# Causal mask in a decoder's self-attention: from a triangle matmul on TensorE to a select on GpSimd, with values held two steps and q and k pieces given out one by one

## The chip, the core and the metric

The kernel runs on one core of a Trainium2 chip. The core has five engines with queues of their own: TensorE (PE, whose weight loads are shown apart as PEld), VectorE (DVE), ScalarE (ACT), GpSimd (POOL) and SyncE (SP), which here issues DMAs. The metric is the time of one execution on the device in microseconds; several executions give a median.

## The reference

A decoder of four layers works on x of shape 8 x 256 x 128 (batch, tokens, features), in float32. Each layer adds self-attention (or another mixer), cross attention to a context, and a feed-forward part with experts. The change concerns attention. Layers 0 and 1 have causal self-attention with 16 heads of 8 features; the core of it:

```python
    scores = jnp.einsum('bhqd,bhkd->bhqk', Q, K) * scale
    causal = jnp.tril(jnp.ones((S, S), dtype=bool))
    scores = jnp.where(causal, scores, NEG_INF)
    weights = jax.nn.softmax(scores, axis=-1)
    attn = jnp.einsum('bhqk,bhkd->bhqd', weights, V)
```

Q and K are turned by rotary tables first. Cross attention of layers 0, 1 and 3 has the same heads; layer 0 masks keys and multiplies the weights by a side input after the softmax (`attn = attn * group_prob[:, None, :, :]`), layer 1 masks keys, layer 3 has neither. Layer 2 has another kind of attention, and the self-attention place of layer 3 is a state-space scan; neither runs the changed functions.

## The kernel before

The work of attention is cut into 40 jobs, a job being one layer and one batch element: eight each of causal layer 0 (`L0a`), cross layer 0 (`L0x`), causal layer 1 (`L1a`), cross layer 1 (`L1x`), cross layer 3 (`L3x`). Layers 0 and 1 go in halves of four batch elements: L0a 0-3, L0x 0-3, L0a 4-7, L0x 4-7, and so for layer 1.

Each job goes through these generators in `main_line`:

- `fronts` and `front` (L666 to L752), for two jobs at once: normalise x, make the rows of q and k (`rows_of`), split each into three bfloat16 pieces whose sum is the float32 value (`pieces`, L641, four GpSimd operations: copy, subtract, copy, subtract), and lay the pieces out by DMA on SP's queue (`spread`, L655) into the tiles `qs` and `ks`. The score matmuls then run on bfloat16 operands of up to 128 rows.
- `pass1` (L800): the score matmuls a first time, mask included, for the row maxima, which DVE reduces from PSUM (L824). GpSimd splits the negated maxima into pieces (`mp`, L831 to L834); PE transposes them (L847), ACT copies them, and SP's queue lays them into further rows of `qs` (`all_maxima`). With these rows the matmuls of the second pass yield score minus maximum.
- `pass2` (L857): keys are now on the partitions. There are eight steps per job: four groups of four heads (`s`), two blocks of 128 keys (`kt`). A step makes banks of 512 scores (L893), takes their exponential on ACT (L901, tile `prob`) and, for `L0x`, multiplies them by the transposed side input into `probw`, in turn on DVE and GpSimd (L906). The value matmuls of a step (`values`, L867) are issued one step later: the step is kept in `held`. In causal jobs the second key block needs the second 128 queries only; in both blocks the first 128 query columns of a bank are the diagonal block. There a matmul of the identity with `tri_k` (L896), a triangle of 0 and -1e30, adds the mask to the scores in PSUM, as `tri_q` does in `pass1` (L818).
- `terms` (L761): loads the masks of cross layers (and the side input), turns a mask into a matmul operand on GpSimd (`mq`, L774 or L776), and transposes it on PE (L758).
- `backs`: normalises and projects out.

The order of work is written out by Python generators, not by the chip. `drive` (L392) emits one unit of `pass1` or of `pass2` at a time; `pass1` leads by about 1.15 job (`LEAD`), and a clock counts the units. The other generators, among them fronts, terms, backs and the experts of other layers (`aside`), advance when their own time has come: `yield us(t)` sets a pause of t microseconds on that clock (`TICK` 0.85 us per unit), a bare `yield` sets 1.8 us. Emission fixes the order in each engine's queue, so a pause moves instructions past others, and takes no time on the chip by itself.

Tiles come from rotating buffers: `sb(shape, tag, bufs)`. `prob` has 6 and `probw` 4, of which `rows_of` takes some for the rotary products. PSUM has three banks for scores of pass 2 (`sc`), two for pass 1 (`s1`), one for the values (`av`), two for everything else (`mm`).

In the experts' part, `sorted_experts`, GpSimd scatters the tokens of half the batch by eight indirect DMAs (L1409) and gathers results by eight more (L1516). Of the six such runs of scatters, three fall into causal stretches.

Of the kernel before, what the change touches and what calls it, by code (L numbers as in the profile page):

```python
# [18 lines left out]
P = 128  # L19
B = 8  # L20
S = 256
# [17 lines left out]
TICK = 0.85  # L39
LEAD = 1.15  # L40
WB = 3
BIG = 1e30


# [203 lines left out]
def kernel(  # L248
# [30 lines left out]
    def sb(shape, tag, bufs, dt=F32):  # L279
        return pools["soft"].tile(list(shape), dt, tag=tag, name=tag, bufs=bufs)  # L280
# [186 lines left out]
    nc.gpsimd.memset(nhalf, -0.5)  # L467

    tri_q = cpool.tile([P, P], BF16, name="tri_q")
    tri_k = cpool.tile([P, P], BF16, name="tri_k")  # L470
    for t, sign in ((tri_q, 1), (tri_k, -1)):
        nc.gpsimd.memset(t, 0.0)
        nc.gpsimd.affine_select(
            out=t, in_=t, compare_op=ALU.is_ge, fill=-BIG, base=0,
            pattern=[[-sign, P]], channel_multiplier=sign)

    sumsel = cpool.tile([P, G], F32, name="sumsel")
    nc.gpsimd.memset(sumsel, 0.0)
# [156 lines left out]
    def main_line(jobs, loads, aside):  # L635
# [5 lines left out]
        def pieces(src, nm):  # L641

            out, rest = [], src
            for i in range(NPC):
                if i:
                    r = sb([P, 2 * S], "qkf", 3) if i < NPC - 1 else sb([P, 2 * S], f"pc{i}", 2, BF16)
                    nc.gpsimd.tensor_tensor(r, rest, out[-1], ALU.subtract)
                    rest = r
                if i < NPC - 1:
                    b = sb([P, 2 * S], f"pc{i}", 2, BF16)  # L650
                    nc.gpsimd.tensor_copy(b, rest)  # L651
                    out.append(b)
            return out + [rest]

        def spread(dst, pcs, of_q, queues):  # L655
# [17 lines left out]
        def front(j, y, b):  # L673
# [12 lines left out]
            def rows_of(n, src):  # L686
                f = sb([P, 2 * S], "qkf", 3)
                if y.rope:
                    parts = []
                    for sw, tab in (("", "cos"), ("s", "sin")):  # L690
                        pp = mm_tile()
                        mm(pp, w["w" + n + sw], src, start=True, stop=True)
                        o = sb([P, 2, S], "probw", 4)
                        pv = pp.rearrange("p (b s) -> p b s", b=2)
                        table = bc(rope[tab + n], 1, 2)
                        if "b" + n in w:
                            nc.vector.scalar_tensor_tensor(o, pv, w["b" + n + sw], table, ALU.add, ALU.mult)
                        else:
                            nc.vector.tensor_tensor(o, pv, table, ALU.mult)
                        parts.append(o)  # L700
                        yield us(1)
                    nc.gpsimd.tensor_tensor(
                        f.rearrange("p (b s) -> p b s", b=2), parts[0], parts[1], ALU.add)
                else:
                    pp = mm_tile()
                    mm(pp, w["w" + n], src, start=True, stop=True)
                    if n == "q":
                        nc.scalar.activation(f, pp, AF.Identity, bias=y.bqs, scale=scale)
                    else:
                        nc.scalar.activation(f, pp, AF.Identity, bias=w["bk"])  # L710
                    yield us(1)
                return pieces(f, n)

            first = j == 0
            if y.cross:
# [141 lines left out]
        def pass2(j, y, b):  # L857

            q, k, v = qss[b // 2 % 2], kss[b // 2 % 2], vflat[b % 4]
            c0 = b % 2 * S  # L860
            yield from wait(("front", j // 2 * 2), ("terms", j))
            _, mk, sideT = y.terms.pop(b, (None, None, None))
            y.avs[b] = []
            held = None
            units, n = 0, NS * T + (12 if y.causal else 16)

            def values(av, s, kt, q0, probs):  # L867
                for sums in ((False, True) if sideT is not None else (False,)):
                    for j in range(4):
                        o = av[G * j : G * (j + 1), s % 2 * S + q0 : s % 2 * S + S]  # L870

                        at = (kt * H + 4 * s + j) * VW
                        mm(o, sumsel if sums else v[:, at : at + G], probs[j][0 if sums else 1],  # L873
                           start=kt == 0 and not sums,
                           stop=kt == T - 1 and sums == (sideT is not None))
                if s % 2 and kt == T - 1:
                    a = sb([P, 2, S], "avs", 2)
                    nc.scalar.copy(a.rearrange("p s q -> p (s q)"), av)  # L878
                    y.avs[b].append(a)

            for s in range(NS):
                yield from wait(("max", j, s // 2))
                if s % 2 == 0:
                    av = av_tile()
                for kt in range(T):
                    q0 = kt * P if y.causal else 0
                    nq = S - q0
                    nh = 512 // nq
                    probs = []
                    for g in range(4 * s, 4 * s + 4, nh):  # L890
                        bank = sc_tile().rearrange("p (a c) -> p a c", a=nh)
                        for a in range(nh):
                            one = mm(bank[:, a, :], k[:, g + a, c0 + kt * P : c0 + (kt + 1) * P],  # L893
                                     q[:, g + a, c0 + q0 : c0 + S], start=a == 0 or y.bare, stop=y.bare)
                        if y.causal:
                            one = mm(bank[:, :, 0:P], identb, bc(tri_k, 1, nh), start=False, stop=True)  # L896
                        elif mk is not None:
                            one = mm(bank, far[y.mask[1]], bc(mk[:, kt, :], 1, nh), start=False, stop=True)  # L898
                        last["pe"] = one
                        p = sb([P, nh, nq], "prob", 6)  # L900
                        last["act"] = nc.scalar.activation(p, bank, AF.Exp)  # L901
                        pw = p
                        if sideT is not None:
                            pw = sb([P, nh, nq], "probw", 4)
                            eng = nc.gpsimd if (g // nh + kt) % 2 else nc.vector
                            eng.tensor_tensor(pw, p, bc(sideT[:, kt, :], 1, nh), ALU.mult)  # L906
                        probs += [(p[:, a, :], pw[:, a, :]) for a in range(nh)]
                        units += 1
                        at["p2"] = j + units / n
                        yield  # L910
                    if held is not None:
                        values(*held)
                    held = (av, s, kt, q0, probs)
                    units += 1
                    at["p2"] = j + units / n
                    yield
            values(*held)
            done.add(("p2", j))

        def backs():  # L920
# [929 lines left out]
```

## Time and profile before

| | |
|---|---|
| three runs | 1709.3, 1717.98, 1718.88 us |
| median | 1717.98 us |
| profiled execution | 1709.84 us |
| its span, first to last instruction | 1708.1 us |
| mean granted TensorE clock | 0.913 |

The parts of the kernel, told apart by when the triangle matmul (L896) runs, follow each other in the span:

| stretch, us | main line of attention |
|---|---|
| 53 to 147 | L0a, batch 0-3 |
| 147 to 292 | L0x, batch 0-3 |
| 292 to 385 | L0a, batch 4-7 |
| 385 to 582 | L0x, batch 4-7 |
| 582 to 681 | L1a, batch 0-3 |
| 681 to 838 | L1x, batch 0-3 |
| 838 to 927 | L1a, batch 4-7 |
| 927 to 1090 | L1x, batch 4-7 |

After that come layer 2, the state space, L3x and the last experts. Stretches overlap by a job or so, since `pass1` runs ahead. Experts of the previous layer run beside the main line from about 290 us on.

How to read the views: a group's line shows the source line, the engine, the operation, the tiles written and read, the count, then the busy time and the mean of one, then the idle time of the engine just before. PE's records overlap, so the distance of two starts tells what a matmul occupies, and its duration does not. The chain of waits goes back from the last instruction through whatever released each step.

### The profile page before, as it was taken

What the parts mean: (1) busy time and instruction counts of PE and PEld (TensorE: products, weight loads), DVE (VectorE), ACT (ScalarE), POOL (GpSimd) and SP (SyncE); (2) the same over time, 40 slices, a digit from 0 to 9 for tenths busy, and PEclk for the clock granted to TensorE, in tenths of its full rate; (3) what the DMA queues carried; (4) which work ended last, traced back from release to release, by engine and by line L of the source; (5) the groups of instructions that cost most, each with busy time, mean ns of one, the idle gap of its engine ahead of it and who ended that gap; (6) DMA issues with size and microseconds to landing.
All of it is one profiled execution on the core that took longest, in us unless ns stands there. A gap on an engine that the chain in (4) does not pass through costs nothing.

```text
span 1708.1 us, 28915 instructions
## 1 busy us (share of the span) xinstructions
PE 1425.3 (83%) x10546; PEld 894.2 (52%) x10546; DVE 949.9 (56%) x2546; ACT 615.2 (36%) x1267; POOL 608.6 (36%) x859
## 2 busy tenths in 40 slices
PE   2897988888879878889989989747977777988997
PEld 1454544556445546545556546446845653554553
DVE  5455766635567553746553656413457455767753
ACT  0352333442324334145434244312332214633551
POOL 3433666421565531242342232132134523342211
PEclk7899999998989989999999999768988888998996
DMA  3332120344301225321136320066410642012000
GB/s 108 91 103 62 50 57 15 119 134 133 93 20 57 62 86 169 100 71 58 58 104 185 103 70 2 2 207 223 150 35 15 192 138 72 13 54 77 8 8 13
DMA packets 113519, 141.64 MB, mean 83 GB/s; under 512 B 12384, under 2 KB 97888, under 8 KB 113248
## 3 DMA queue, kind: packets, MB, share of 16 engines
q1 hardware_dynamic: 94064, 121.33, 23.2%
q10 hardware_dynamic: 16240, 12.17, 2.4%
q0 software_dynamic: 3072, 6.30, 1.2%
q8 instruction: 83, 1.36, 0.4%
q14 instruction: 60, 0.49, 0.1%
HBM read 79.53 MB, written 12.06 MB: 54 GB/s over the span
## 4 chain that ended last, share of the span: by engine, by line
PE 58%; DVE 11%; POOL 10%; DMA 7%; issue 7%; ACT 3%; SPq 2%; another core or an unknown queue 0%; POOLq 0%; ACTq 0%; DVEq 0%
PE av L873 9%; PE s L815 6%; PE sc L1494 6%; PE sc L893 6%; DVE neg L824 4%; PE mm L1464 4%; PE s L821 2%; DMA qs<-pc 2%; PE sc L898 2%; DMA r_w<-in_w_L_big_dram 2%; POOL r_x L1516 2%; POOL probw L906 2%; PE mm L502 2%; SPq L661 2%; PE mm L933 2%
## 5 line engine op out<-in xcount | busy, mean ns | idle before, releaser
L824 DVE TENSOR_REDUCE neg<-s 128x2 f32<-128x512 f32 (+1 forms) x576 | 387.2, 683 | 218.6 <-PE s L818 82.7
L901 ACT ACTIVATE prob<-sc 128x512 f32<-128x512 f32 x576 | 336.4, 597 | 376.9 <-PE sc L898 197.4
L815 PE MATMUL s<-ks,qs 125*128 125x256 bf16 (+1 forms) x1280 | 236.9, 274 | 95.0 <-DVE neg L824 58.4
L893 PE MATMUL sc<-qs,ks 128*128 128x256 bf16 (+1 forms) x1280 | 229.1, 270 | 4.7 <-DMA qs<-mT 4.4
L815 PEld LDWEIGHTS <-qs 125*128 125x128 bf16 x1280 | 113.6, 102 | 201.8 <-issue 147.3
L1494 PE MATMUL sc<-r_xT,r_w 128*128 128x128 f32 x720 | 162.4, 319 | 35.2 <-ACT r_h L1497 10.6
L873 PE MATMUL av<-prob,vpad 128*32 128x256 f32 (+1 forms) x2048 | 168.3, 368 | 10.1 <-ACT prob L901 8.9
L893 PEld LDWEIGHTS <-ks 128*128 128x128 bf16 x1280 | 111.2, 100 | 98.0 <-issue 65.8
L1494 PEld LDWEIGHTS sc<-r_xT,r_w 128*128 128x128 f32 x720 | 114.9, 203 | 79.0 <-ACT r_h L1497 35.9
L1499 DVE TENSOR_SCALAR r_h<-sc,r_w 128x128 f32<-128x128 f32 x180 | 62.7, 350 | 143.7 <-PE sc L1494 109.0
L651 POOL CAST pc<-qkf 128x512 bf16<-128x512 f32 x80 | 51.8, 648 | 217.3 <-ACT qkf L710 155.1
L1497 ACT ACTIVATE r_h<-sc,r_w 128x128 f32<-128x128 f32 x180 | 65.9, 368 | 153.1 <-PE sc L1494 122.7
L1464 PE MATMUL mm<-r_w,r_h 128*128 128x128 f32 x600 | 105.4, 293 | 1.0 <-DVE r_h L1499 0.9
L906 POOL TENSOR_TENSOR probw<-prob,sideT 128x512 f32<-128x512 f32 x64 | 84.3, 1318 | 48.8 <-ACT prob L901 48.5
L831 POOL CAST mp<-neg 128x16 bf16<-128x16 f32 x80 | 19.8, 247 | 222.6 <-DVE neg L824 219.1
L1464 PEld LDWEIGHTS mm<-r_w,r_h 128*128 128x128 f32 x600 | 88.0, 204 | 7.4 <-DVE r_h L1499 2.9
L873 PEld LDWEIGHTS av<-prob,vpad 128*32 128x32 f32 x2048 | 47.2, 109 | 81.0 <-issue 45.3
L577 POOL TENSOR_TENSOR ln_rs<-ln_rs,nhalf 128x4 f32<-128x4 f32 x40 | 43.3, 1085 | 113.5 <-DVE ln_rs L576 112.7
L878 ACT COPY avs<-av 128x512 f32<-128x512 f32 x80 | 46.9, 586 | 84.6 <-PE av L873 58.8
L906 DVE TENSOR_TENSOR probw<-prob,sideT 128x512 f32<-128x512 f32 x64 | 56.4, 881 | 27.6 <-ACT prob L901 18.1
L873 PE MATMUL av<-probw,vpad 128*32 128x256 f32 x512 | 53.3, 403 | 22.1 <-POOL probw L906 21.8
L1516 POOL DMA_INDIRECT r_x<-ysorted,r_sloti x48 | 46.5, 969 | 60.7 <-DMA r_x<-xsorted 45.4
(408 smaller groups left out, 2575.4 us busy)
## 6 DMA issues: line engine op xcount, KB each, us to landing
r_w<-in_w_L_big_dram SPq DMA_DIRECT2D x60, 578.0 KB
ks<-pc SPq DMA_DIRECT2D x177, 128.0 KB
qs<-pc SPq DMA_DIRECT2D x177, 128.0 KB
r_w<-in_w_L_big_dram SPq DMA_DIRECT2D x30, 579.0 KB
r_x<-xsorted SPq DMA_DIRECT2D x18, 256.0 KB
ysorted<-r_y SPq DMA_DIRECT2D x18, 256.0 KB
mi<-in_mask_dram ACTq DMA_DIRECT2D x16, 256.0 KB
qs<-mT SPq DMA_DIRECT2D x160, 6.0 KB
```

The costliest lines, as they stand in the source:

```text
L651: nc.gpsimd.tensor_copy(b, rest)
L815: one = mm(bank[:, a, :], q[:KM, g + a, c0 + qt * P : c0 + (qt + 1) * P], k[:KM, g + a, c0 : c0 + nk], start=a == 0 or y.bare, stop=y.bare)
L824: last["dve"] = nc.vector.tensor_reduce(neg[:, qt, g - h0 : g - h0 + nh], bank, AX.X, ALU.max, negate=True)
L873: mm(o, sumsel if sums else v[:, at : at + G], probs[j][0 if sums else 1], start=kt == 0 and not sums, stop=kt == T - 1 and sums == (sideT ...
L893: one = mm(bank[:, a, :], k[:, g + a, c0 + kt * P : c0 + (kt + 1) * P], q[:, g + a, c0 + q0 : c0 + S], start=a == 0 or y.bare, stop=y.bare)
L901: last["act"] = nc.scalar.activation(p, bank, AF.Exp)
L906: eng.tensor_tensor(pw, p, bc(sideT[:, kt, :], 1, nh), ALU.mult)
L1464: mm(py, hid[:, f, :], wt[:, w2 : w2 + D], start=f == 0, stop=f == NF - 1)
L1494: mm(o, wt[:, f * P : (f + 1) * P], xT[:, i, :], start=True, stop=True)
L1497: nc.scalar.activation(hid[:, f, :], o, AF.Relu, bias=bias)
L1499: nc.vector.tensor_scalar(hid[:, f, :], o, bias, 0.0, ALU.add, ALU.max)
L1516: nc.gpsimd.indirect_dma_start(yg[:, i, :], None, ysort, bass.IndirectOffsetOnAxis(ap=sloti[:, at : at + 1], axis=0))
```

## The change

The change does five things:

- In `pass2` of causal jobs the matmul with `tri_k` goes, and so does `tri_k`; every score matmul is an accumulation group of its own. After the exponential, GpSimd's `affine_select` overwrites, in place, the entries of the diagonal block whose key is behind the query position by 0.
- `pass2` holds two steps (`HELD = 2`) before it issues a step's value matmuls, in all layers; what is held is issued at the end of the job.
- `prob` gets 8 buffers instead of 6, `probw` 6 instead of 4.
- `pieces` becomes a generator which pauses for 1.4 us on the clock after each of its four operations.
- The start of an accumulation group is worded by `mk is None` instead of `y.bare`; for cross layers that comes to the same.

The pass for the maxima keeps its triangle.

```diff
+HELD = 2
@@ constants
     tri_q = cpool.tile([P, P], BF16, name="tri_q")
-    tri_k = cpool.tile([P, P], BF16, name="tri_k")
-    for t, sign in ((tri_q, 1), (tri_k, -1)):
-        nc.gpsimd.memset(t, 0.0)
-        nc.gpsimd.affine_select(
-            out=t, in_=t, compare_op=ALU.is_ge, fill=-BIG, base=0,
-            pattern=[[-sign, P]], channel_multiplier=sign)
+    nc.gpsimd.memset(tri_q, 0.0)
+    nc.gpsimd.affine_select(
+        out=tri_q, in_=tri_q, compare_op=ALU.is_ge, fill=-BIG, base=0,
+        pattern=[[-1, P]], channel_multiplier=1)
@@ pieces
                     nc.gpsimd.tensor_tensor(r, rest, out[-1], ALU.subtract)
                     rest = r
+                    yield us(1.4)
                 if i < NPC - 1:
                     b = sb([P, 2 * S], f"pc{i}", 2, BF16)
                     nc.gpsimd.tensor_copy(b, rest)
                     out.append(b)
+                    yield us(1.4)
@@ rows_of
-                        o = sb([P, 2, S], "probw", 4)
+                        o = sb([P, 2, S], "probw", 6)
...
-                return pieces(f, n)
+                return (yield from pieces(f, n))
@@ pass2
-            held = None
+            held = []
...
-                                     q[:, g + a, c0 + q0 : c0 + S], start=a == 0 or y.bare, stop=y.bare)
-                        if y.causal:
-                            one = mm(bank[:, :, 0:P], identb, bc(tri_k, 1, nh), start=False, stop=True)
-                        elif mk is not None:
+                                     q[:, g + a, c0 + q0 : c0 + S],
+                                     start=a == 0 or mk is None, stop=mk is None)
+                        if mk is not None:
                             one = mm(bank, far[y.mask[1]], bc(mk[:, kt, :], 1, nh), start=False, stop=True)
                         last["pe"] = one
-                        p = sb([P, nh, nq], "prob", 6)
+                        p = sb([P, nh, nq], "prob", 8)
                         last["act"] = nc.scalar.activation(p, bank, AF.Exp)
                         pw = p
+                        if y.causal:
+                            nc.gpsimd.affine_select(
+                                out=p[:, :, 0:P], in_=p[:, :, 0:P], compare_op=ALU.is_ge, fill=0.0, base=0,
+                                pattern=[[0, nh], [1, P]], channel_multiplier=-1)
                         if sideT is not None:
-                            pw = sb([P, nh, nq], "probw", 4)
+                            pw = sb([P, nh, nq], "probw", 6)
...
-                    if held is not None:
-                        values(*held)
-                    held = (av, s, kt, q0, probs)
+                    held.append((av, s, kt, q0, probs))
+                    if len(held) > HELD:
+                        values(*held.pop(0))
...
-            values(*held)
+            while held:
+                values(*held.pop(0))
```

## The prediction

> **What bounds the kernel now.** I read the busy table first, then the slices by stage, then the chain of waits, then the waits of TensorE and GpSimd.
>
> ```profile
> PE 1425.3 (83%) x10546; PEld 894.2 (52%) x10546; DVE 949.9 (56%) x2546; ACT 615.2 (36%) x1267; POOL 608.6 (36%) x859
> PE 58%; DVE 11%; POOL 10%; DMA 7%; issue 7%; ACT 3%; SPq 2%; another core or an unknown queue 0%; POOLq 0%; ACTq 0%; DVEq 0%
> ```
>
> TensorE (PE) is the busiest engine and 58% of the chain; no other engine fills its time. The rest of the chain is hops to VectorE (DVE), GpSimd (POOL) and DMA. The triangle matmul (L896) runs in four stretches only, the self-attention jobs with a causal mask; busy time by engine in each (columns: busy us and count for PE, PEld, DVE, ACT, POOL, then granted clock, DMA):
>
> ```profile
> 53.00:147.00 94.00, 80.27 (x696) 46.89 (x696) 38.79 (x89) 39.90 (x77) 30.67 (x51) 0.93 0.38 111
> 292.00:385.00 93.00, 78.46 (x734) 52.66 (x731) 48.30 (x144) 41.03 (x86) 28.48 (x47) 0.96 0.41 123
> 582.00:681.00 99.00, 85.11 (x779) 56.90 (x777) 50.23 (x153) 41.89 (x88) 29.15 (x47) 0.95 0.42 128
> 838.00:927.00 89.00, 76.07 (x681) 50.85 (x678) 38.56 (x113) 38.07 (x82) 25.10 (x40) 0.92 0.41 124
> 147.00:292.00 145.00, 126.56 (x1056) 67.55 (x1053) 100.10 (x202) 48.05 (x91) 90.96 (x107) 0.98 0.12 36
> ```
>
> The first four are causal: 375 us, POOL busy 113.4 us of it. The last is cross attention of layer 0, where POOL also makes half of the weighted exponentials (L906). There PE waits for POOL, and the chain of that last stretch runs through it:
>
> ```profile
> by line: PE av L873 15.0%; issue 12.0%; POOL probw L906 11.2%; PE s L815 7.3%; PE sc L893 5.7%; DVE neg L824 5.3%; PE sc L898 5.1%; PE s L821 4.8%; POOL pc L651 3.4%; POOL qkf L647 3.1%; POOL qkf L702 2.6%; PE mm L692 2.6%; PE mm L502 1.8%;
> ```
>
> The waits of PE over the whole span say the same (total us, times, longest):
>
> ```profile
> PE av L873 <- POOL probw L906: 21.8, 18, 3.2
> PE av L873 <- ACT prob L901: 8.9, 13, 4.3
> ```
>
> **The change part by part.** The sum is against the profiled execution: 1709.84 us, span 1708.1. The median of the three runs shown, 1717.98, is 8.1 us above it.
>
> *1. The triangle leaves PE: -21 us.* The groups give 192 matmuls 61.2 us of busy time (128 of 256 columns at 284 ns, 64 of 512 at 387 ns). That is not what they occupy. Matmuls overlap, as their start times show:
>
> ```profile
> 94.02 0.39 PE L893 MATMUL sc<-qs,ks 128*128 128x256 bf16 x2
> ...
> 94.25 0.27 PE L896 MATMUL sc<-tri_k,identb 128*128 128x256 bf16 x1
> ...
> 94.36 0.38 PE L815 MATMUL s<-ks,qs 125*128 125x256 bf16 x2
> ```
>
> The triangle starts at 94.25 and the next matmul at 94.36: 0.11 us, where its record says 0.27. The chain counts a 512-column one as 0.22. So 128 x 0.107 + 64 x 0.215 = 27.5 us of PE. Added up along the chain of waits, L896 is 6.9 + 3.1 + 5.3 + 4.9 us in the four stretches and 1.0 elsewhere: 21. I take 21, bounds 0 (another wait takes its place) and 27.5. Its 192 weight loads (100 ns) lie beside matmuls.
>
> *2. Selects on POOL: 99 us of POOL work, +8 us on the path.* There are 12 per causal job, 192 in all: 128 over 2x128 elements, 64 over 512, in place, between the exponential and its value matmuls. The trace has one-off selects of 128 columns at 295 ns, none larger. Nearest row for how a one-input POOL operation grows: CAST of 16 elements 198 ns (median), of 512, 611 ns. Grown like that, 295 ns becomes about 0.40 and 0.61; grown in proportion, 0.59 and 1.18. I take 0.42 and 0.70: 128 x 0.42 + 64 x 0.70 = 99 us (bounds 90 and 151). POOL in the causal stretches goes from 113 to 212 of 375 us, so its load does not end them; lateness can.
>
> [...] The rows above decide for me: POOL is idle 262 us of these stretches, so only the wait counts.
>
> The cover is the PE work between the last score matmul of a bank and the first value matmul that reads it. I counted it in the order of instructions of both programs (0.1 us per 256-column pass, f32 two passes). Before, values run one step late; after, two (HELD = 2). Median cover in causal jobs goes from 2.85 to 3.65 us, the lowest tenth from 1.2 to 1.56. The need is 0.95 us (exponential 0.60, PE drain, signals), after 1.5 to 1.8. Summing need minus cover where positive: 1.6 us before, 10.1 after: +8.5, mostly at ends of jobs, where both held steps are flushed. Bounds 0 and 20 (dearest select).
>
> *3. Selects queued behind POOL work that waits: +7 us.* POOL takes its queue in order. Two kinds of work stand ahead of selects:
>
> ```profile
> 323.47 1.24 POOL L1409 DMA_INDIRECT xsorted<-r_rows,r_sloti  x1 [3.89 <-DVE r_sloti L1404]
> ...
> 341.75 1.51 POOL L774 TENSOR_SCALAR mq<-mi 128x512 bf16<-128x512 int32 x1 [7.12 <-DMA mi<-in_mask_dram]
> ```
>
> Eight scatters in a row (L1409) last 10.1 us, in three of the four stretches. In the changed order three selects follow them directly; about 5.3 us of PE work lies between the scatters' start and the first values that need one, so PE stalls some 5 us. But PE already stalls there: 4.2 us for POOL mp L834, 4.3 us (ACT prob) and 5.4 us (DVE neg) at the three places. Net +1 each: +3. The mask preparation (L774, L776) waits for a mask transfer; 8 of its 16 lie in causal stretches, with 37.8 us of POOL idle before them. A select behind one comes about 4.7 + 1.7 us late against 3.65 us of cover, but PE reaches the transposes of the same mask, which wait for it too (L758, 7.4 us in all before): +0.5 each, +4. Bounds for both together: -3 and +40. In turn a select waits for its exponential, and behind it on POOL stand the parts of the maxima (L831 to L834), for which PE's transpose (L847) waits; a select comes in the order after its exponential (0.60 us), and pass 2 uses those maxima about a job later: 0, at most +5.
>
> *4. HELD = 2 and six probw buffers in layer 0's cross attention: -20 us.* Cover goes from 4.6 to 6.9 us (lowest tenth 3.2 to 4.4). The need is one POOL product (1.32 us) plus what is queued before it, up to five piece operations, 0.61 + 1.16 + 0.61 + 1.16 + 1.32. PE waits 21.8 us for probw, its weight loads 31.6; two more us of cover exceed most single waits (longest 3.2). I take 20, bounds 5 and 31. Cover if this fails: DVE, busy 100 of 145 us, would be the next late one.
>
> *5. HELD = 2 in the other cross layers: -4 us.* ACT prob waits at values are 8.9 us on PE; outside the causal stretches the weight loads have 11 (28.4 less 17). Bounds 0 and -8.
>
> *6. Pieces one by one: 0.* Four pauses of 1.4 us per row set let other POOL work in between; no instruction is added. The key and query transfers on SP's queue still start when the buffers come free two jobs later; between last piece and first use lie several us of PE work in both orders. POOL mp behind pieces becomes earlier. Bounds -6 and +10; what would be late next is pass 1's first score matmul, which waits 22.4 us for qs<-pc already. Eight prob buffers instead of six keep two free with one more step held, as before: 0. One memset and one select fewer at the start (0.5 us) lie beside input transfers: 0.
>
> Sum: -21 + 8 + 7 - 20 - 4 + 0 = -30, so 1680 on the profiled execution's scale and 1688 on the median's.
>
> **The rivals.**
>
> *A. Gain cancelled (1712).* In cross attention DVE ends the steps instead of POOL, so part 4 gives 5 and part 5 nothing, and part 1 gives 16 (5 of its 21 turn into other PE waits): -16 - 5 + 15 = -6. For it: DVE 69% busy there. Against: the waits of the values name POOL, not DVE (1.8 us).
>
> *B. Slower: the select's queue becomes the bound (1757).* At 11 places in causal stretches (8 mask waits, 3 scatter runs) values wait for a select behind POOL. If PE's earlier stalls there do not cover it, a mask place costs 6.8 - 2.7 = 4 us and a scatter place 5 to 10: 32 + 24 = 56, with the dearer selects +20, against -21 of part 1 and -16 of parts 4 and 5: +39. It decides once the mean loss at these 11 places exceeds (21 + 20 + 4 - 8)/11 = 3.4 us. For it: in-order POOL and its 7 us waits. Against: the PE stalls already there.
>
> *C. Larger gain (1651).* All POOL pieces of the chain in cross attention (probw 30 us, qkf and pc 25) go with the longer cover: -27 - 55 + 15 = -67. Against: PE waited only 22 to 32 us for it.
>
> That the selects are not issued, or that the values are not two steps late, is excluded: the changed order shows both.
>
> **How the numbers follow.** Likeliest 0.66, 1688, own range 1668 to 1706; A 0.10; B 0.16; C 0.08. About 1% (17 us) is what a measurement of this kernel can tell. Faster by over 1% is under 1700.8: 0.58 of the likeliest and C, 0.66. Within 1%: 0.08 of the likeliest, A, and a weak B: 0.18. Slower: 0.16. The range 1655 to 1725 leaves out half of C and most of B.
>
> **What would show it.** Right: no L896; a select of about 0.42 and 0.70 us; PE's wait for POOL probw under 8 us; causal stretches shorter by 3 to 5 us each, cross attention of layer 0 by about 10 per half. Part 2 or 3 is wrong if values wait more than 25 us for selects. The forecast fails if such waits stand at most of the 11 places, or if probw waits stay near 22 us.

## The result, and the profile after

| | before | changed |
|---|---|---|
| median of 10 runs each, same chip | 1718.43 us | 1739.19 us |
| lowest and highest | 1709.3, 1729.01 | 1727.63, 1741.36 |
| ratio, 95% interval | | 1.0118, 1.009 to 1.0147 |
| profiled execution, span | 1708.1 | 1733.5 |
| granted TensorE clock | 0.913 | 0.909 |

The changed kernel is slower by some 20 us, where a gain of 30 us was forecast; 1739 us lies outside the forecast's 1655 to 1725. The busy table and the chain of the changed kernel:

```profile
PE 1415.8 (82%) x10354; PEld 889.3 (51%) x10354; DVE 954.5 (55%) x2546; ACT 611.6 (35%) x1267; POOL 695.8 (40%) x1049
...
PE 53%; DVE 13%; POOL 12%; DMA 9%; issue 7%; ACT 3%; SPq 2%; another core or an unknown queue 1%; POOLq 0%; ACTq 0%; DVEq 0%
```

The 192 triangle matmuls are gone, yet PE is busy only 9.5 us less, while its idle time (span less busy) went from 283 to 318 us. PE's share of the chain fell by five points, and DMA, DVE and POOL took them. The groups of the select and PE's waits (total, times, longest) in the changed kernel:

```profile
L905 POOL TENSOR_SCALAR_AFFINE_SELECT prob<-prob 128x256 f32<-128x256 f32 (+1 forms) x192 | 91.4, 484 | 140.9 <-ACT prob L901 135.3 <-DMA r_w<-in_w_L_big_dram 2.2 <-PE sc L1500 2.0
```

```profile
PE av L874 <- POOL probw L911: 23.1, 12, 8.5
PE av L874 <- POOL prob L905: 23.1, 17, 3.8
PE s L816 <- DMA qs<-pc: 18.1, 3, 13.4
...
PE s L816 <- DMA xsorted<-zero: 8.7, 1, 8.7
```

A select has one of two shapes; taken apart, the 128 smaller ones take 408 ns each on average and the 64 larger ones 634. The selects cost GpSimd about what was forecast (91 us for 99). Two waits don't fit: the one for the products (L911, L906 before), which two held steps were to bring under 8 us, is 23.1 with a new longest of 8.5; and pass 1 waits 8.7 us in one place for what the profile calls the zero fill of `xsorted`, a transfer of the experts' part.

Where the time went shows best by stage. A stage ends with the last copy of its values (`avs`) in ScalarE's timeline; the durations from these marks, in us (the two last columns are experiments below):

| stage | before | changed | pauses only | one late pause |
|---|---|---|---|---|
| L0a 0-3 | 132.2 | 153.1 | 151.6 | 150.6 |
| L0x 0-3 | 159.7 | 145.9 | 153.4 | 153.3 |
| L0a 4-7 | 100.4 | 100.1 | 95.4 | 97.4 |
| L0x 4-7 | 187.9 | 188.0 | 197.5 | 196.5 |
| L1a 0-3 | 97.9 | 104.2 | 99.1 | 101.0 |
| L1x 0-3 | 149.2 | 154.2 | 156.0 | 156.5 |
| L1a 4-7 | 100.0 | 99.3 | 102.7 | 103.2 |
| L1x 4-7 | 154.7 | 169.7 | 174.4 | 170.3 |
| rest, to the last L3x | 575.9 | 568.5 | 567.0 | 570.9 |

The loss sits in a few stages, the first and the last of layers 0 and 1 above all, not in the causal ones evenly. The selects run alike in all four causal stages, and two of these have hardly changed.

### The profile page after: what moved, and what is told of

The parts are those of the page before. It is cut to its first block, busy times and chain, and to the rows that moved or that the text cites. A ratio compares the mean times of both kernels' runs of the same rounds, so it can differ in the third digit from the quotient of the medians.

```text
span 1733.5 us, 28759 instructions
## 1 busy us (share of the span) xinstructions
PE 1415.8 (82%) x10354; PEld 889.3 (51%) x10354; DVE 954.5 (55%) x2546; ACT 611.6 (35%) x1267; POOL 695.8 (40%) x1049
## 4 chain that ended last, share of the span: by engine, by line
PE 53%; DVE 13%; POOL 12%; DMA 9%; issue 7%; ACT 3%; SPq 2%; another core or an unknown queue 1%; POOLq 0%; ACTq 0%; DVEq 0%
PE av L874 9%; PE sc L894 6%; PE sc L1500 5%; PE s L816 5%; DVE neg L825 5%; PE mm L1470 3%; POOL probw L911 2%; DMA qs<-pc 2%; DMA r_w<-in_w_L_big_dram 2%; PE sc L898 2%; PE mm L501 2%; PE s L822 2%; PE mm L939 2%; DMA mi<-in_mask_dram 2%; POOL r_x L1522 1%
## 5 line engine op out<-in xcount | busy, mean ns | idle before, releaser
L901 ACT ACTIVATE prob<-sc 128x512 f32<-128x512 f32 x576 | 331.7, 597 | 319.3 <-PE sc L898 150.8
L816 PE MATMUL s<-ks,qs 125*128 125x256 bf16 (+1 forms) x1280 | 239.8, 277 | 94.2 <-DVE neg L825 36.6
L874 PE MATMUL av<-prob,vpad 128*32 128x256 f32 (+1 forms) x2048 | 178.8, 374 | 32.6 <-POOL prob L905 23.1
L905 POOL TENSOR_SCALAR_AFFINE_SELECT prob<-prob 128x256 f32<-128x256 f32 (+1 forms) x192 | 91.4, 484 | 140.9 <-ACT prob L901 135.3
L1470 PE MATMUL mm<-r_w,r_h 128*128 128x128 f32 x600 | 111.7, 292 | 2.5 <-DVE r_h L1505 2.2
L874 PEld LDWEIGHTS av<-prob,vpad 128*32 128x32 f32 x2048 | 54.6, 111 | 106.3 <-issue 48.2
L911 POOL TENSOR_TENSOR probw<-prob,sideT 128x512 f32<-128x512 f32 x64 | 87.2, 1367 | 39.7 <-ACT prob L901 39.6
L1522 POOL DMA_INDIRECT r_x<-ysorted,r_sloti x48 | 46.9, 976 | 63.3 <-DMA r_x<-xsorted 45.6
L911 DVE TENSOR_TENSOR probw<-prob,sideT 128x512 f32<-128x512 f32 x64 | 59.7, 942 | 19.9 <-ACT prob L901 12.3
```

Of the source, the lines that this page charges most:

```text
L816: one = mm(bank[:, a, :], q[:KM, g + a, c0 + qt * P : c0 + (qt + 1) * P], k[:KM, g + a, c0 : c0 + nk], start=a == 0 or y.bare, stop=y.bare)
L905: nc.gpsimd.affine_select(out=p[:, :, 0:P], in_=p[:, :, 0:P], compare_op=ALU.is_ge, fill=0.0, base=0, pattern=[[0, nh], [1, P]], channel_m ...
L1470: mm(py, hid[:, f, :], wt[:, w2 : w2 + D], start=f == 0, stop=f == NF - 1)
L1522: nc.gpsimd.indirect_dma_start(yg[:, i, :], None, ysort, bass.IndirectOffsetOnAxis(ap=sloti[:, at : at + 1], axis=0))
```

## The experiments

Each ratio is against the kernel before on the same chip, with its 95% interval. Two theories stood at first. Theory S: the selects come late for the values. Theory O: the new order of work (pauses in the pieces, two held steps) is what costs.

**The triangle left out, nothing in its place** (keys behind the query count in pass 2).

```diff
-                        if y.causal:
-                            one = mm(bank[:, :, 0:P], identb, bc(tri_k, 1, nh), start=False, stop=True)
-                        elif mk is not None:
+                        if mk is not None:
```

> The kernel before, with the triangle matmul of the second pass left out and nothing in its place: keys behind the query stay in the exponentials, so this part of the mask is left out of the computation. It measures what the triangle costs on PE. My prediction's term: 21 us faster than before, 0.988. Theory S (the selects' lateness ate the gain): the same, about 0.985 to 0.990, since the triangle is on the path. Theory O (the new order of work loses it): also 0.985 to 0.990. If PE's triangle were hidden behind other waits: 0.998 to 1.002.

Measured: 1.0005 (0.9983 to 1.0027). The matmuls that the forecast's largest term is about are worth nothing.

**The selects instead of the triangle in the order of before**: one held step, no pauses; the change's `affine_select` is the only new line.

> The kernel before, with selects in place of the triangle matmul, values still one step late, no pauses, old buffer counts. Against the kernel without either mask it shows what the selects cost in the old order. Theory S: 25 us or more over that kernel, so 1.00 to 1.01 of before, and value matmuls wait over 30 us for selects. Theory O: under 12 us over that kernel, 0.99 to 0.995 of before.

Measured: 1.0109 (1.0083 to 1.0135). Against the kernel without a triangle that is 18 us for the selects, between what the two theories asked for (25 or more, under 12). PE's wait for them is over 30 us, as theory S had it:

```profile
PE av L873 <- POOL prob L903: 37.9, 28, 4.0
```

**The changed kernel without its selects** (no mask in pass 2): the `affine_select` is deleted.

> The changed kernel with its selects left out, all else (two steps, buffers, pauses) kept: keys behind the query stay in the exponentials. Theory S: the selects carry the loss, so 35 us or more faster than the changed kernel, about 0.985 of before. Theory O: the order itself is slow, so still 1.00 to 1.01 of before, and PE's 8.5 us wait for the weighted exponentials behind the gathers (at 460 to 470 us) is still there.

Measured: 1.0042 (1.0021 to 1.0063). The selects are 0.76% or 13 us of the changed kernel; with them away, and with them the triangle, it is still 7 us slower than before, and PE's longest wait for a product is still 8.4 us, as theory O had it. Both theories hold a part.

**The pauses alone** in the kernel before.

```diff
                     nc.gpsimd.tensor_tensor(r, rest, out[-1], ALU.subtract)
                     rest = r
+                    yield us(1.4)
...
                     out.append(b)
+                    yield us(1.4)
...
-                return pieces(f, n)
+                return (yield from pieces(f, n))
```

> The kernel before with the pauses between the pieces of q and k alone; triangle, one step and buffers as before. No instruction is added. My prediction's term: 0, that is 0.997 to 1.003. Theory O: a loss of 8 us or more (1.005 or above), with PE waiting for q and k layouts behind the zero fill at the start, or for work behind the gathers. Theory S: 1.000.

Measured: 1.0191 (1.0164 to 1.0218), 33 us. The step forecast at 0 is the dearest of all.

**The second held step alone**, with its buffers.

```diff
-            held = None
+            held = []
...
-                    if held is not None:
-                        values(*held)
-                    held = (av, s, kt, q0, probs)
+                    held.append((av, s, kt, q0, probs))
+                    if len(held) > HELD:
+                        values(*held.pop(0))
```

> The kernel before with one part of the change alone: the values of two steps held back instead of one, with eight buffers for the exponentials and six for their products. The triangle stays, no selects, no pauses; the order on SyncE's queue is that of before. In the last batch the pauses alone cost 33 us, and the change without its selects cost 7: between these two lie the second held step and the triangle, together some -25. Theory R (the second held step only repairs what the pauses break: it gives the values slack for products that come late): the ratio is 0.997 to 1.003. Theory G (it is a gain of its own, as the prediction had it with -24 us in its fourth and fifth step: TensorE's wait for the products in the first cross layer falls from 21.8 us): 0.985 to 0.993.

Measured: 0.9922 (0.9895 to 0.9948), 1694.85 us: a gain of its own of 13 us, and faster than both kernels. PE's wait for the products here:

```profile
PE av L874 <- POOL probw L907: 13.8, 10, 4.2
```

That is 8 us less than the 21.8 of before.

**The change without its pauses.**

> The changed kernel with its selects and the two held steps, but the pieces of q and k given out in one go as before. If the pauses are what costs (theory P: they put the layouts of q and k later on SyncE's queue and let the gathers in front of the products), this is faster than the changed kernel by 15 to 30 us and near the kernel before: ratio 0.995 to 1.005, TensorE's wait for the layouts of q back under 10 us. If the selects are what costs (theory S, 13 to 18 us measured with and without them) and the pauses only in the absence of the second held step, it is as slow as the changed kernel: ratio 1.008 to 1.014.

Measured: 0.9985 (0.9957 to 1.0012). Theory P: the pauses cost 1.33% or 23 us inside the change. The rest of the expectation was wrong: the wait for the layouts didn't fall (32.5 us here, 18.1 in the changed kernel). A shorter wait is no proof of an earlier transfer; an engine that reaches its wait later waits less. By stage the gain lies where the loss was: the first stage takes 139.7 us (153.1 with the pauses) and the last of layers 0 and 1 154.9 (169.7). What the selects wait for shows in two timelines of this kernel in its third stage, GpSimd's and then PE's (start, duration, what, idle before it):

```profile
327.63 1.24 POOL L1413 DMA_INDIRECT xsorted<-r_rows,r_sloti  x1 [0.33 <-DVE r_sloti L1408]
329.17 0.97 POOL L1413 DMA_INDIRECT xsorted<-r_rows,r_sloti  x1 [0.30 <-issue]
...
336.77 0.96 POOL L1413 DMA_INDIRECT xsorted<-r_rows,r_sloti  x1 [0.30 <-issue]
337.75 0.77 POOL L903 TENSOR_SCALAR_AFFINE_SELECT prob<-prob 128x256 f32<-128x256 f32 x2
```

```profile
338.22 1.43 PE L872 MATMUL av<-prob,vpad 128*32 128x256 f32 x8 [6.46 <-POOL prob L903]
```

Eight scatters hold GpSimd for 10 us, the select stands behind them, and PE idles 6.46 us for it; 6.35 and 5.89 at the two like places. Over the span PE's wait for the selects is:

```profile
PE av L872 <- POOL prob L903: 40.4, 20, 6.5
```

**The triangle twice.** The same matmul is issued once more ahead of it.

> The kernel before with the triangle's matmul of the second pass issued twice (the mask is twice as large, its exponential is 0 all the same): TensorE gets what the change takes away, 27 us of occupancy, in the same places. The prediction's first step puts 21 of such 27 us on the path. Leaving the triangle out gained nothing (ratio 1.0005). Theory of slack (in the causal stretches something other than TensorE's work sets the end, or what the engine saves it loses in the granted clock): between 0.998 and 1.005 here. Theory of a floor (TensorE's work did bound these stretches before, and without the triangle something just behind it took its place): 1.010 to 1.017.

Measured: 1.0016 (0.9986 to 1.0046): 3 us (-2 to +8) for 27.5 us more of PE occupancy. With the triangle left out and with it doubled the time stays, so some 27 us of PE work more or less in these stages does not move the end. Idle time of PE and its clock can both have a part in that (see the last section). The windows on the causal stretches of the forecast (columns as there), first without the triangle, then with two:

```profile
53.00:147.00 94.00, 76.76 (x636) 43.55 (x636) 36.62 (x83) 39.49 (x77) 30.54 (x51) 0.90 0.38 111
292.00:385.00 93.00, 76.69 (x677) 47.14 (x678) 45.96 (x140) 39.45 (x83) 31.86 (x52) 0.93 0.35 104
582.00:681.00 99.00, 79.91 (x725) 50.77 (x723) 49.70 (x148) 40.85 (x86) 32.25 (x53) 0.92 0.37 112
838.00:927.00 89.00, 73.68 (x646) 47.81 (x645) 41.18 (x122) 37.76 (x80) 26.86 (x45) 0.90 0.42 125
```

```profile
53.00:147.00 94.00, 83.24 (x734) 49.69 (x734) 36.97 (x83) 40.10 (x77) 30.61 (x51) 0.95 0.38 111
292.00:385.00 93.00, 83.04 (x746) 54.70 (x746) 47.10 (x138) 39.16 (x81) 28.68 (x48) 0.93 0.34 106
582.00:681.00 99.00, 86.31 (x791) 57.25 (x787) 50.09 (x145) 40.59 (x84) 29.41 (x48) 0.95 0.37 113
838.00:927.00 89.00, 83.07 (x757) 55.97 (x756) 44.08 (x128) 38.97 (x82) 26.88 (x45) 0.96 0.42 128
```

In the kernel before, the four windows held 2890 matmuls and 319.9 us of busy PE. Without the triangle they hold 2684: 206 fewer, of which the triangles are up to 192, so the same 375 us took in no other work in their place. PE was busy 12.9 us less, not 27.5, and idle 12.9 us more. The granted clock fell in all four (0.93, 0.96, 0.95, 0.92 before).

**The pauses charged at 0.2 us** instead of 1.4.

> The kernel before with the pieces of q and k given out one by one, but each pause charged at 0.2 us instead of 1.4, so that the next piece follows one step of the attention later instead of two. A front has eight such pauses, so its layouts are asked for some 7 us of work later than before instead of some 13. If lateness of the layouts is the cost (theory P), the loss shrinks with it: ratio 1.005 to 1.012 against the 1.019 of the long pauses. If it is the new order as such (one piece's place among the products and gathers on GpSimd), the loss isn't in proportion: 1.015 or more, or any sign.

Measured: 1.01 (1.0064 to 1.0136). About half the delay (7 us of work per front for 13), about half the loss.

**One late pause**: the pieces in one go, and one pause behind them. It is as long as the four together: 1.4 us on a clock of 0.85 us per unit takes two units, so four pauses take eight, or 6.8 us.

```diff
-                return pieces(f, n)
+                out = pieces(f, n)
+                yield us(6.8)
+                return out
```

> The kernel before with the pieces of q and k given out in one go, and one pause behind them of the four pauses' whole length (6.8 us of work), ahead of the copies that lay the pieces out for TensorE. Theory of lateness: what the pauses cost is that these copies are asked for later on SyncE's queue, and it does not matter where the pieces themselves stand: ratio 1.014 to 1.024, as with the four pauses (1.019), and the first causal stage again some 10 to 20 us longer. Theory of interleaving: it is the pieces, spread out on GpSimd among products, gathers and maxima, that make others late; then without the spreading little is left: 0.997 to 1.006.

Measured: 1.0206 (1.0166 to 1.0245), as the four pauses, and stage by stage within 4.1 us of them (table above). So it does not matter that the pieces are apart: a later call for the copies into `qs` and `ks` is enough for the whole loss. SyncE's timeline in the first causal stage (start, us from the first issue's start to the last one's end, what, count), before and then with the four pauses:

```profile
69.47 1.93 SPq L661 DMA_DIRECT2D qs<-pc  x3
71.50 1.53 SPq L852 DMA_DIRECT2D qs<-mT  x2
73.14 8.91 SPq L661 DMA_DIRECT2D qs<-pc  x6
```

```profile
78.80 1.93 SPq L663 DMA_DIRECT2D qs<-pc  x3
80.83 1.53 SPq L854 DMA_DIRECT2D qs<-mT  x2
82.47 11.74 SPq L663 DMA_DIRECT2D qs<-pc  x6
```

The pieces were ready at 66.1 and at 68.4 us (end of the last L647 in GpSimd's timeline). The last of their copies was issued at 82.0 and at 94.2. PE's timeline with the four pauses, the wait ahead of each row in brackets:

```profile
83.73 0.59 PE L895 MATMUL sc<-qs,ks 128*128 128x256 bf16 x2 [6.22 <-DMA qs<-mT]
...
98.66 0.58 PE L817 MATMUL s<-ks,qs 125*128 125x128 bf16 x4 [5.08 <-DMA mi<-in_side_dram]
```

The 2.3 us on GpSimd became 12.2 on SyncE, and pass 1 of the second pair begins at 98.66 instead of 85.12. The maxima of the first pair (`qs<-mT`) stand behind the copies and are issued at 80.83 instead of 71.50; pass 2 waits 6.22 us for them. Among the copies of pieces in this stretch the longest hold of SyncE, with the four pauses, was this:

```profile
SPq L663 <- DMA w_L_ffn<-in_w_L_ffn_dram: 6.4, 1, 6.4
```

So the profile puts that hold down to a load of expert weights; before, the longest hold of such a copy here was 4.8 us, for a load of `x`. In the last stage of layer 1 SyncE's timeline shows the same, before and then with the four pauses:

```profile
977.40 6.21 SPq L661 DMA_DIRECT2D qs<-pc  x9
...
985.28 0.42 SPq L441 DMA_DIRECT2D w_L_attn<-in_w_L_attn_dram  x1
985.75 0.42 SPq L441 DMA_DIRECT2D w_L_xattn<-in_w_L_xattn_dram  x1
```

```profile
1025.35 0.49 SPq L441 DMA_DIRECT2D w_L_attn<-in_w_L_attn_dram  x1
1025.89 0.42 SPq L441 DMA_DIRECT2D w_L_xattn<-in_w_L_xattn_dram  x1
...
1027.12 12.48 SPq L663 DMA_DIRECT2D qs<-pc  x6
```

Before, all nine copies of q went ahead of the next layers' weights and took 6.2 us to issue; with pauses six follow the weights and take 12.5, and PE waits 7.91 us (0.45 before). How a load holds SyncE the profile doesn't tell.

**Pauses in the causal fronts only**, and **in the cross fronts only**: `pieces` gets an argument `gap`, true for `y.causal` or `y.cross`, around its two yields.

> The kernel before with the four pauses in the fronts of the causal layers alone. In the run with all pauses the first causal stage was 19 us longer, the other three causal stages together 1 us; its second pair's layout of q was asked for at 92 us instead of 79, and the last block of its maxima at 81 instead of 72. If that front causes it (theory: the second pair's layouts are asked for behind a later step of the attention, and the first pair's maxima stand behind them on SyncE's queue), this run shows the same 15 to 20 us in the first stage and part of it is won back in the first cross stage (6 there): ratio 1.005 to 1.012. If the stage was lengthened by the cross layer's first keys, whose pieces are given out in the same stretch: 0.998 to 1.003.

> The kernel before with the four pauses in the fronts of the cross layers alone. With all pauses the first cross job of the second half of the first layer took 10 us more and the second cross job of the last such stage 17 us more (its layouts were asked for behind the big transfers of the expert stage). By the theory that each front's loss is its own, this run shows these two, the first causal stage within 5 us of before, and with pauses_causal it adds up to the 33 us of all pauses: ratio 1.008 to 1.015. If the cross fronts alone carry the loss: 1.016 to 1.022. If they carry none: within 0.003 of 1.

Measured: 1.0046 (1.0014 to 1.0079) and 1.0154 (1.0115 to 1.0193), together 2.0% for the 1.9 of all; the first is a shade under its expected range, the second a shade over. Causal pauses lengthen the first stage to 164.3 us, of which all but 10 are back by the end of the first cross stage. Cross pauses carry three quarters of the loss; there the first stage is only 3.7 us longer, but the first job of the first cross stage another 5.6, and of the two late places expected, the first L0x job of the second half loses 18 us (part of it won back) and the second L1x job of the last such stage 14. The sum fits, but not stage by stage: in the first stage the two add 32 and 4 us, and all pauses together only 19. So the theory that each front's loss is its own is not borne out; that the totals add up may be luck.

**VectorE instead of GpSimd for the mask**, in the change without pauses: a product with a triangle of ones (`tri_k` is that triangle now, in float32).

```diff
-                            nc.gpsimd.affine_select(
-                                out=p[:, :, 0:P], in_=p[:, :, 0:P], compare_op=ALU.is_ge, fill=0.0, base=0,
-                                pattern=[[0, nh], [1, P]], channel_multiplier=-1)
+                            nc.vector.tensor_tensor(p[:, :, 0:P], p[:, :, 0:P], bc(tri_k, 1, nh), ALU.mult)
```

> The change with its second held step, without its pauses, and with the selects replaced: VectorE multiplies the diagonal blocks of the exponentials by a triangle of ones and zeros instead of GpSimd selecting. Beside it stand the same kernel with the selects (ratio 0.9985) and the one that keeps TensorE's triangle (0.9922); the selects cost 6 to 7 us in each of the four causal stages. If it is GpSimd's queue (the selects behind scatters, pieces and mask work) that makes them late, VectorE does better: 0.988 to 0.995. If it is the added step as such between the exponential and the values, whatever engine does it, or VectorE's own load in these stages (the maxima of the next pass 1 wait behind the products): 0.996 to 1.006.

Measured: 0.9979 (0.9951 to 1.0008), the same as with selects. PE's wait for the masked exponentials, 40.4 us with the selects, is here:

```profile
PE av L877 <- DVE prob L907: 13.0, 16, 2.5
```

No time came of these 27 us: other waits of PE grew, for the parts of the maxima (`mp`, 1.8 to 13.8 us) and for the maxima from VectorE (`neg`, 47.4 to 55.0). So taking the mask off GpSimd's queue gains nothing here. Whether the added step as such is the price, or VectorE's own load took the place of GpSimd's queue, this run does not separate.

**Two held steps and no mask in pass 2** (the selects of the change without pauses deleted; keys behind the query count).

> The change without its pauses and without its selects: the second held step, and no triangle in the second pass (keys behind the query count in it). Beside it the same with the triangle (0.9922) and with the selects (0.9985). If the removal of the triangle is worth nothing in this order either, as it was with one held step (1.0005), and the added step costs: 0.989 to 0.994. If with two held steps TensorE's work does bound the causal stages, so that the 21 us of the prediction are there: 0.978 to 0.985, and the selects cost twice what I count. If the freed time even harms (TensorE idles more and its clock is granted less): 0.995 to 1.000, and the selects cost nothing.

Measured: 0.9915 (0.9883 to 0.9947), against 0.9922 with the triangle. Its removal is worth nothing in this order too, and the selects cost 0.70% or 12 us beside it.

**A third held step in the causal layers**, in the change without pauses.

```diff
-                    if len(held) > HELD:
+                    if len(held) > HELD + y.causal:
```

> The change without its pauses, and in the causal layers three held steps instead of two (the buffers as in the change). If the selects cost by their delay alone, which now exceeds what two held steps cover, a third covers it, TensorE's wait for them falls from 95 us in both of its rows to under 40, and the four causal stages lose their 6 to 7 us each: ratio 0.989 to 0.995. If the wait only moves to the end of each job, where all held steps are given out, or the maxima of the next pass wait instead: 0.996 to 1.003.

Measured: 0.999 (0.9965 to 1.0015), no gain. PE's wait for the selects stays:

```profile
PE av L872 <- POOL prob L903: 37.1, 17, 6.9
```

A third step doesn't cover a row of scatters, and at a job's end all held steps are given out anyway. This doesn't tell which of the two.

**The buffers only**: `prob` 8 for 6, `probw` 6 for 4.

> The kernel before with eight buffers for the exponentials and six for their products instead of six and four, one step held as before. If TensorE's and ScalarE's waits for free buffers are part of what the second held step gains (0.9922), some of it is here: 0.993 to 0.997. If the held step is what gains, because values of the last step no longer wait for products of that step: 0.998 to 1.002.

Measured: 0.9968 (0.9943 to 0.9993). Of the 13 us of the held step with its buffers some 5 are the buffers'.

**Fronts hurried**: the second held step, and the pauses that the fronts had already cut to 0.2 us.

```diff
                 if len(queues) == 1:
-                    yield us(2)
+                    yield us(0.2)
...
                         parts.append(o)
-                        yield us(1)
+                        yield us(0.2)
```

> The second held step alone (0.9922), and the pauses that the fronts have already cut down: 0.2 us instead of 2 between the copies of a layout, and 0.2 instead of 1 between the two rotary products, so that a front gives its layouts out some 9 us of work earlier. If lateness of the layouts is priced both ways (33 us for 14 us of pause per front): a gain beside 0.9922, 0.975 to 0.988. If the fronts of the kernel before are just early enough, or the copies now stand in front of the maxima's copies on SyncE's queue: 0.990 to 1.005.

Measured: 1.0033 (1.0009 to 1.0056), 19 us above the held step alone. PE's waits:

```profile
PE mm L848 <- POOL mp L835: 33.3, 7, 5.7
...
PE sc L894 <- DMA qs<-mT: 19.6, 3, 6.6
```

Without the hurry these two waits were 15.4 and 4.4 us. That copies given out sooner stand in front of those of the maxima on SyncE would fit the second; the first is a wait for GpSimd's split of the maxima, and its cause was not looked for. In this kernel earlier is no better than later.

**The scatters one by one**, 2 us apart, in the change without pauses.

```diff
-            if t % 4 == 3:
-                yield us(4)
+            yield us(2)
```

> The change without its pauses (0.9985), with the eight scatters of each routing step given out one by one, 2 us of work apart, instead of in two groups of four with 4 us behind each: in the three causal stages where they stand in front of selects, at most three now stand together. If the row of scatters is what makes the selects cost (three waits of TensorE of 6 us each), these waits fall under 3 us and the ratio goes to 0.988 to 0.994. If the time is bound elsewhere in these stages, as it was when VectorE multiplied instead (waits shorter by 27 us, time the same), the waits fall and the ratio stays within 0.996 to 1.001. The later end of the scatters could also delay the expert stage: 1.002 or more.

Measured: 1.0081 (1.0049 to 1.0113). The longest wait for a select fell from 6.5 to 2.3 us and all of them from 40.4 to 25.2, yet the kernel is 16 us slower. The edit changed more than it was meant to: the third stage went from 101 to 86 us and the fourth from 182 to 201, so that work of other parts seems to have moved from one to the other. What the scatters cost on the path stays open.

**The changed kernel with one held step.**

> The changed kernel with one held step instead of two, its buffers as they are (eight and six). Pauses alone cost 1.9 per cent, selects alone 1.1, and the buffers alone gain 0.3: if these add up and the second held step only gains its share of 0.5 per cent as it did alone, 1.018 to 1.026. If the second held step is worth more here, because both parts make the products and exponentials late for the values: 1.027 to 1.036. If it is worth nothing here: 1.010 to 1.014, as the changed kernel (1.012).

Measured: 1.0266 (1.0235 to 1.0296). The second held step is worth 1.48% or 25 us inside the change, twice the 13 us of step and buffers together in the kernel before. That it hides part of the lateness that the rest brings would explain it; this was not tested.

## Why the prediction was wrong, by its own steps

From the kernel before in three measured moves: held steps and buffers -0.78%, the selects for the triangle on top +0.63, the pauses on top +1.33, in all +1.18. In us of the median of before: -13, +11 and +23, in all +20 before rounding, each to about 6 (two intervals of 0.27% combined), against the forecast's -30.

- **Step 6, pieces one by one, 0 us (bounds -6 to +10): failed; it is +23, and +33 alone.** It said that the copies "still start when the buffers come free two jobs later" and that several us of PE work lie between last piece and first use. The run with one late pause refutes it: copies given out later were issued later (the last of q at 94.2 us for 82.0, with four pauses), and the work behind them had no slack for that (pass 1 of the second pair at 98.66 for 85.12). The step named what would be late next, pass 1's first score matmul behind `qs<-pc`, and then priced it at nothing, since SyncE's queue was not followed past the edit.
- **Step 1, the triangle, -21 (bounds 0 to -27.5): failed; it is 0** (-3 to +5 us alone, -1 with about 7 either way beside two held steps). The chain of waits counts 21 us on L896 rightly, but a chain says what was last, not what comes next when it goes. The prediction's own windows held a warning: in the four causal stretches PE is idle for 55 us (375 less 319.9). Without the triangle 12.9 us of busy time became idle time there. Which wait took its place, and how much the lower clock took back, stays open.
- **Steps 2 and 3, selects, +15: right in size**, 18, 12 and 13 us in three settings. One select took 0.41 and 0.63 us for the 0.42 and 0.70 taken. The stalls behind the scatters were forecast at some 5 us each and are 6.5, 6.4 and 5.9 in the change without pauses. That this queue makes the price is not shown, since VectorE is no cheaper; the size may be right by luck.
- **Steps 4 and 5, held steps, -24: too large for the kernel before (-13, of it 5 from buffers), near in size inside the change (-25 for the step without its buffers), by luck: the sum was made for a kernel without lateness from pauses.** The place was half right. Alone, PE's wait for the products fell from 21.8 to 13.8 us, not under 8. In the changed kernel it is 23.1, and 13.4 (longest 4.2) without the pauses. With them, gathers of the experts (L1522) stand ahead of a product on GpSimd, as the timeline of the changed kernel shows:

```profile
468.10 1.44 POOL L1522 DMA_INDIRECT r_x<-ysorted,r_sloti  x1 [0.16 <-issue]
469.84 0.94 POOL L1522 DMA_INDIRECT r_x<-ysorted,r_sloti  x1 [0.30 <-DVE x L1533]
470.81 1.27 POOL L911 TENSOR_TENSOR probw<-prob,sideT 128x512 f32<-128x512 f32 x1
```

  Seven of the eight ran ahead of it from 460.56 on, and PE waited 8.5 us for that product, the new longest.

Rival B was right in sign and wrong in cause: it made the select's queue the bound, while the selects do not outweigh the held steps: with both, and without pauses, the kernel stands at 0.9985.

## What to carry to other kernels

In a program that writes out its order, a pause takes no engine's time and still sets when a DMA is asked for (here the last copy of q 12.2 us later): before calling it free, follow the copies behind it on their queue and see what they will now meet. A matmul's time on the chain of waits is no forecast of what its removal gains: here 21 us on the chain were worth nothing. Leaving it out and doubling it are two cheap runs that tell. A part of a change that gains should be run alone: the second held step, without the rest, is the fastest version here (0.9922).

## What was not expected of the hardware

PE's mean granted clock was lower without the triangle and higher with two. Over all runs, each beside the kernel before on the same chip: without the triangle 0.910 (12 runs, 0.907 to 0.915) for 0.914 (23 runs, 0.906 to 0.920); with the triangle twice 0.922 (12 runs, 0.917 to 0.928) for 0.915 (30 runs, 0.910 to 0.920). Read in windows of 1 us, the clock of the kernel before is 1.00 in 1380 of 1708 windows, 0.50 in 265 and between the two in 63; of the changed kernel it is 1.00 in 1382 of 1733, 0.50 in 287 and between in 64. Every window between has 1.00 on one side and 0.50 on the other. What makes it change, these windows don't show.

If the runs compared here all have these two values alone, the time at 0.50 is twice the span times what the mean clock lacks to 1. As an estimate on that condition, from the spans and means of the runs, it is 293 us before and 308 without the triangle, and 291 before and 267 with two: some 27 us of extra matmuls came with about 24 us less at 0.50. The mean clocks of the causal stretches agree in direction without the triangle (0.90 to 0.93, for 0.92 to 0.96 before); with two they are 0.93 to 0.96, higher in two of the four, the same in one and lower in one. This may be part of why removed PE work bought nothing; how much of it, these runs do not separate from the waits.
